# A decoder layer with routed experts on one core: shared experts of three batches moved into the last sorting, first group's tiles and joins moved forward

## The chip, the core and the metric

One core of a Trainium2 chip runs the whole kernel in one launch. The metric is device time in microseconds. The engines are named as the profile names them: PE (TensorE, the matrix engine), DVE (VectorE), ACT (ScalarE), POOL (GpSimd) and SP (SyncE, which here only issues DMAs). Each engine works through its own instructions in order; waits between engines go through semaphores.

## The reference, cut to what matters

Eight batches of 512 tokens with 256 features, float32. Three sublayers, each with a layernorm before it and a residual add behind it:

```python
x = x + attn(layernorm(x))            # one weight vector per head, rolled over the rows, causal
x = x + xattn(layernorm(x), ctx, ctx) # causal softmax attention over a context
x = x + ffn(layernorm(x))

# ffn, on tokens t:
out     = sum over 2 shared experts of (silu(x @ wg_s) * (x @ wu_s)) @ wd_s
probs   = softmax(x @ router_w)                       # 16 routed experts
weights = the two largest of probs, normalized to sum 1
out    += sum over the two chosen experts e of weight_e * (silu(x @ wg_r[e]) * (x @ wu_r[e])) @ wd_r[e]
```

The batches are independent of each other everywhere. The change touches only the order of work in the last sublayer, and some buffers.

## The kernel before, in words

**Batches.** A loop over the eight batches emits, for batch b, the "back" of b (attention's products, projection, second layernorm, scores, softmax, attention, third layernorm, logits, router), interleaved by a list written out by hand (`ORDER`) with the "front" of b + 1 and with what is left of b - 1: its shared experts (steps `h0`, `h1`, `d0`, `d1`, from `steps_shared`), its ranking (`rk`) and its sends (`sd0` to `sd7`). `shared[b]` ends with the residual held in a buffer `x`; for batches of the first group it is also stored to DRAM (`kept`).

**Routing.** The batches form two groups, `GROUPS = ((0, 1, 2, 3, 4), (5, 6, 7))`. For each batch, `ranked` (`rk`) works out on DVE the row that each token takes in its expert's list, and each `send` (L588) is one scatter by POOL of 128 rows to a list in DRAM, `xg`. After the last batch of a group, `tiled` and `tabled` build on DVE and PE the table of tiles of 128 rows: which rows, which expert (`row0`, `far`, `col`). This stretch, from the ranking of the last batch to the first tile loads, is "the sorting".

**Quads.** The routed experts are computed in quads of four tiles, 14 quads for the first group and 10 for the second (`steps_routed`). A quad q is made of: `fetch` (SP loads four tiles, L718), `pick` (ACT copies the gate and up weights of the four tiles' experts, SP and ACT load the down weights `wdn`, L737), `turn` (PE transposes), `hidden` (L772), `down` (L786, then the results `y` times the routing weight on ACT and DVE), and four `put`s (L807), scatters by POOL to `yg` in DRAM. `quads[q]` is a list for a software pipeline: it holds `pick` and `turn` of q + 1, `hidden` of q, `down` of q - 1, `fetch` of q + 3 (q + 4 in the second group), two puts of q - 1 and two of q - 2. So there are two entries more than quads, 16 for the first group.

**Joins.** When all puts of a group are done, `steps_join` makes the output for each batch: `keep` loads the stored residual (`xj`, L842; the first group only), `take` loads the two results of each token (`yj`, L851, two loads of 512 KB), `join` adds both on DVE (L860, two adds over 128 x 1024) and stores to `out` (L861). The buffers of `keep` alternate between two tags with one buffer each (`xn1`, `ctxT`); those of `take` have the tags `qT` and `v2`, two buffers each, so two batches can be in flight.

**Where the quads and joins lie.** `merged` interleaves lists evenly, each step at its share of its list; `idle(n)` puts n empty steps into a list to shift what is behind them. The first group's quads 0 to 11 are merged into the steps of batches 5, 6 and 7 (`lead` is 5): entries 0 to 4, 5 to 8, and 9 to 11. Behind the loop, the sorting of the second group is merged with the remaining entries 12 to 15, the shared experts of batches 6 and 7, and the first six steps of the first group's joins. The rest of those joins is merged with the second group's quads, and the joins of the second group come last. The emitted order is not the final one on each engine: the framework's scheduler orders the instructions anew within the limits of data and buffers, but stays near the emitted order.

Of the kernel before, what the change touches and what calls it, by code (L numbers as in the profile page):

```python
# [25 lines left out]
NSH = 2  # L26

GROUPS = ((0, 1, 2, 3, 4), (5, 6, 7))

XW = D + 2  # L30
FAR = float(1 << 16)
# [41 lines left out]
def decoder_layer(ctx: ExitStack, tc: tile.TileContext, x, ctxT, waT, wvT, woT, bo, wkT, xwv, wqT, wr, wg, wu, wd, out):  # L73
# [634 lines left out]
    def steps_routed(g):  # L708
# [13 lines left out]
        def pick(q):  # L722
            def f():
                wgu = sb.tile([P, QT, 2, KC, MR], F32, tag="wgu", bufs=2, name=f"wgu{g}_{q}")
                es = loaded(G, "act", mybir.EngineType.Activation, G["col"][:, q * QT:(q + 1) * QT], (NE - 1) * MR)
                for i, e in enumerate(es):
                    G["act"] = nc.scalar.copy(wgu[:, i], wgu_r[:, :, :, bass.ds(e, MR)]).ins  # L727

                wdn = sb.tile([P, QT // 2, D], F32, tag="wdn", bufs=3, name=f"wdn{g}_{q}")
                for eng, name, engine, i0, cols in (  # L730
                    (nc.scalar, "act", None, 2, es[2:]),
                    (nc.sync, "sp", mybir.EngineType.SP, 0, G["col"][:, q * QT:q * QT + 2]),
                ):
                    if engine is not None:
                        cols = loaded(G, name, engine, cols, (NE - 1) * MR)
                    for i, e in enumerate(cols):
                        G[name] = eng.dma_start(out=wdn[i * MR:(i + 1) * MR, i0 // 2, :], in_=wdn_d[bass.ds(e, MR), :]).ins  # L737
                G["wgu", q], G["wdn", q] = wgu, wdn
            return f
# [94 lines left out]
    def steps_join(g):  # L834
# [10 lines left out]

        def take(bi):
            def f():
                y = [sb.tile([P, NT, D], F32, tag=tag, name=f"yj{GROUPS[g][bi]}_{tag}") for tag in ("qT", "v2")]
                for r in range(2):
                    rows = r * G["n"] + bi * S  # L850
                    nc.sync.dma_start(out=y[r], in_=G["yg"][rows:rows + S, :].rearrange("(p c) d -> p c d", c=NT))  # L851
                G["yj", bi] = y
            return f
# [30 lines left out]
    def iteration(b):  # L884
# [8 lines left out]
        ends = b == GROUPS[0][-1]  # L893
        order = ORDER.split() + (["rk", *[f"sd{i}" for i in range(8)]] if ends else [])

        late = ("-h0", "-h1", "-d0", "-d1") if b == B - 1 else ()
        return [x[n] for n in order if n in x and n not in late and not (b == GROUPS[1][0] and n[:3] in ("-rk", "-sd"))]

    def flat(x):
        return [f for y in x for f in y]  # L900
# [2 lines left out]
    old = [keeps[0], takes[0]]  # L903
    for i in range(len(keeps)):
        if i + 1 < len(keeps):
            old += [keeps[i + 1], takes[i + 1]]
        old.append(joins[i])
    lead = GROUPS[0][-1] + 1
    for b in range(B):
        if b + 2 < B:  # L910
# [2 lines left out]
        if b == lead:  # L913
            now = merged(now, first[:1] + idle(4) + first[1:-1] + idle(18) + first[-1:] + flat(quads[:5]))
        elif b == lead + 1:
            now = merged(now, flat(quads[5:9]))
        elif b == lead + 2:
            now = merged(now, flat(quads[9:12]))
        for f in now:
            f()  # L920
        if b == 0:
            load_blank()
        if b == 1:
            load_experts()
    last, sh6, sh7 = backs[B - 1], shared[B - 2], shared[B - 1]
    send = [last[f"sd{i}"] for i in range(8)]
    gap = flat(quads[12:])
    sh = [x[n] for x in (sh6, sh7) for n in ("h0", "h1", "d0", "d1")]
    sorting = [last["rk"], *idle(1), *send, first1[0], *idle(0), *first1[1:-1], *idle(2), first1[-1]]
    for f in merged(sorting, gap + sh, [*idle(6), *old[:6]]):  # L930
        f()
    keeps, takes, joins = steps_join(1)
    for f in merged(flat(quads1), old[6:]):
        f()
    for f in [*keeps, *takes, *joins]:
        f()


# [52 lines left out]
```

## Time and profile before

| | |
|---|---|
| three runs | 575.97, 581.40, 585.55 us, median 581.4 |
| the profiled execution | 578.12 us, of which 576.4 us are the span of its instructions |
| PE busy | 508.3 us, 88% of the span |
| DVE busy | 373.1 us, 65% |
| ACT busy | 190.9 us, 33% |
| POOL busy | 229.2 us, 40% |
| DMA | 106.62 MB, on average 185 GB/s |
| mean granted clock of PE | 0.954 of full speed |

The share of busy time is an average over stages with different limits. The stages at issue are the last ones. Times from the span's start: the ranking and sorting of the second group lie between about 449 and 476 us, its quads between 484 and 551 us, its puts between 498 and 558 us, and its joins from 559 us to the end.

A row of a group reads: line, engine, operation, what is written from what, count, then busy time, mean duration in ns of one, and the idle time of the engine just before them with what ended it. A row of a timeline reads: start, duration, engine, line, operation, and in brackets the idle time before it and what ended that. "SPq" and "ACTq" are DMA issues of SP and ACT.

### The profile page before, as it was taken

The page shows a single profiled execution, that of the slowest core. Times are in us where ns is not written, and L with a number is a line of the kernel's source. Part 1 is how long each engine was busy: PE and PEld are TensorE (multiplying, and loading weights), DVE is VectorE, ACT ScalarE, POOL GpSimd, SP SyncE. Part 2 cuts the span into 40 slices and gives each one's busy share as a digit, 9 for nine tenths or more (in the row PEclk, how much of TensorE's full clock was granted, in tenths as well). Part 3 has the DMA queues.
Part 4 walks back from the last instruction along what each step waited for, and adds up shares of the span by engine and source line. Part 5 has one row for each costly group of instructions (what it writes and reads, how often), then busy time and mean ns, then how long its engine had stood idle before and what let it go on. Part 6 is the DMA issues. An engine that isn't in the chain of part 4 may idle for free. (4 is left out here: it accounts for less than half of the span.)

```text
span 576.4 us, 10034 instructions
## 1 busy us (share of the span) xinstructions
PE 508.3 (88%) x3172; PEld 335.4 (58%) x3172; DVE 373.1 (65%) x1290; ACT 190.9 (33%) x483; POOL 229.2 (40%) x257
## 2 busy tenths in 40 slices
PE   7989988999999999999799999999898978977810
PEld 5546626756666665673566757676555645845610
DVE  4358749868769768787577568764865753645325
ACT  2233213332332324231445344443333311635300
POOL 3300504432440540634205363743275671357650
PEclk9999999999999999999799999999999979979855
DMA  8870370851580391294359574496221147788947
GB/s 275 278 300 4 94 281 28 276 211 57 169 325 40 138 340 75 104 314 182 105 158 334 171 236 124 129 327 194 89 103 63 43 155 220 249 252 261 280 129 285
DMA packets 63820, 106.62 MB, mean 185 GB/s; under 512 B 8869, under 2 KB 37551, under 8 KB 63666
## 3 DMA queue, kind: packets, MB, share of 16 engines
q1 hardware_dynamic: 51528, 83.35, 44.1%
q0 software_dynamic: 7680, 16.87, 8.1%
q10 hardware_dynamic: 4560, 5.77, 3.0%
q8 instruction: 25, 0.41, 0.3%
q14 instruction: 27, 0.22, 0.1%
HBM read 81.82 MB, written 33.85 MB: 201 GB/s over the span
## 5 line engine op out<-in xcount | busy, mean ns | idle before, releaser
L807 POOL DMA_INDIRECT yg<-y,to x96 | 96.5, 1006 | 101.2 <-ACT y L797 61.5
L240 POOL TENSOR_TENSOR rs<-ve,power 128x2 f32<-128x2 f32 x48 | 35.3, 743 | 173.7 <-DVE ve L239 173.5
L588 POOL DMA_INDIRECT xg<-row,place x64 | 64.9, 1013 | 24.9 <-issue 16.5
L398 PE MATMUL pc<-T,vh 128*32 128x256 f32 (+1 forms) x512 | 57.8, 490 | 3.7 <-DMA T<-zd 2.3
L772 PE MATMUL pgu<-xsT,wgu 128*64 128x128 f32 x768 | 55.1, 285 | 4.6 <-DVE rh L776 3.2
L772 PEld LDWEIGHTS pgu<-xsT,wgu 128*64 128x64 f32 x768 | 44.2, 141 | 15.8 <-issue 12.7
L450 PE MATMUL psc<-kT,qT 128*128 128x128 f32 (+3 forms) x128 | 40.4, 440 | 0.7 <-DVE kT L261 0.7
L225 DVE BATCH_NORM_STATS2 bn<-x 128x6 f32<-128x256 f32 x96 | 37.6, 413 | 4.2 <-DMA x<-in_x_dram 3.2
L479 PE MATMUL pa<-v,pT 128*128 128x256 f32 x160 | 40.3, 382 | 0.0
L786 PE MATMUL py<-wdn,rh 64*128 64x256 f32 x192 | 35.7, 437 | 5.2 <-DMA wdn<-wdn_d 4.8
L398 PEld LDWEIGHTS pc<-T,vh 128*32 128x32 f32 x512 | 18.5, 109 | 35.1 <-issue 19.7
L631 PE MATMUL pd<-wd_sb,h 128*128 128x256 f32 x128 | 36.1, 412 | 3.2 <-DVE h L619 2.3
L338 PE MATMUL pv<-wv_sb,xr 128*128 128x272 f32 (+1 forms) x128 | 34.1, 413 | 4.0 <-ACT xr L331 4.0
L727 ACT COPY wgu<-wgu_r 128x256 f32 x96 | 32.7, 403 | 11.6 <-DVE col L706 7.6
L479 PEld LDWEIGHTS pa<-v,pT 128*128 128x128 f32 x160 | 29.1, 190 | 10.7 <-issue 4.0
L753 PE MATMUL pxt<-ident,xs 128*128 128x128 f32 x192 | 29.6, 284 | 5.8 <-DMA xs<-xg 3.3
L244 DVE TENSOR_SCALAR xn<-x,mv,rs 128x256 f32<-128x256 f32 x64 | 28.1, 476 | 7.2 <-POOL rs L240 6.4
L799 DVE TENSOR_SCALAR y<-py,w 128x256 f32<-128x256 f32 x48 | 22.3, 478 | 15.6 <-ACT y L797 14.5
L614 PE MATMUL pg<-x2T,wg_sb 128*128 128x512 f32 x64 | 31.6, 598 | 0.0
L338 PEld LDWEIGHTS pv<-wv_sb,xr 128*128 128x128 f32 x128 | 24.7, 199 | 10.5 <-ACT xr L331 6.1
L614 PE MATMUL pu<-x2T,wu_sb 128*128 128x512 f32 x64 | 30.4, 592 | 0.0
L354 PE MATMUL pq<-ctxT,qk_sb 128*128 128x512 f32 x64 | 30.4, 594 | 0.0
(174 smaller groups left out, 911.9 us busy)
## 6 DMA issues: line engine op xcount, KB each, us to landing
T<-zd SPq DMA_DIRECT2D x32, 1024.0 KB
xs<-xg SPq DMA_DIRECT2D x96, 129.0 KB
x<-in_x_dram SPq DMA_DIRECT2D x8, 512.0 KB
ctxT<-in_ctxT_dram SPq DMA_DIRECT2D x8, 512.0 KB
yj_qT<-yg SPq DMA_DIRECT2D x8, 512.0 KB
yj_v<-yg SPq DMA_DIRECT2D x8, 512.0 KB
xg<-blank SPq DMA_DIRECT2D x6, 516.0 KB
wdn<-wdn_d ACTq DMA_DIRECT2D x48, 64.0 KB
```

The costliest lines, as they stand in the source:

```text
L225: nc.vector.bn_stats(stats["bn"][:, c, :], src[:, c, :])
L240: st[b].setdefault(("pow", n), []).append(nc.gpsimd.tensor_tensor(stats["rs"][:, lo:hi], ve[:, lo:hi], power[:, lo:hi], ALU.pow).ins)
L338: nc.tensor.matmul(pv[:, :w], xr[:, k, i, :], wv_sb[:, k, :w], start=(k == 0), stop=(k == KC - 1))
L398: nc.tensor.matmul(s["pc"][o][32 * g:32 * g + 32, 2 * jp * P:], vh[:, jp, h, :], s["T"][h // HPT][:, h % HPT, :S - 2 * jp * P], start=(jp ...
L450: nc.tensor.matmul(pc[:, :w], s["qT"][:, k, i * P:w], s["kT"][:, k, :w], start=(k == 0), stop=(k == KC - 1))
L479: nc.tensor.matmul(pa[:, :D], s["pT", i][:, j * P:(j + 1) * P], s["v2"][:, j, :], start=(j == 0), stop=(j == i))
L588: ins = nc.gpsimd.indirect_dma_start(out=grp[g]["xg"][:, :], out_offset=bass.IndirectOffsetOnAxis(ap=s["place"][:, r, c:c + 1], axis=0), i ...
L614: nc.tensor.matmul(p, w[:, k, mt * P:(mt + 1) * P], s["x2T"][:, k, :], start=(k == 0), stop=(k == KC - 1))
L631: nc.tensor.matmul(pd[:, i, :], s["h", mt][:, c * P:(c + 1) * P], wd_sb[:, mt, :], start=(mt == 0), stop=(mt == NSH - 1))
L772: nc.tensor.matmul(p[o * MR:(o + 1) * MR, n, j, :], wgu[:, i, n, k, :], xT[:, k, i, :], start=(k == 0), stop=(k == KC - 1))
L786: nc.tensor.matmul(py[o][:, j, :], h[o * MR:(o + 1) * MR, j, :], wdn[o * MR:(o + 1) * MR, j, :], start=True, stop=True)
L807: ins = nc.gpsimd.indirect_dma_start(out=G["yg"][:, :], out_offset=bass.IndirectOffsetOnAxis(ap=G["to", q][:, i:i + 1], axis=0), in_=G["y" ...
```

## The change

Five things change in the order and two in the buffers.

1. The shared experts of batch 5 no longer run in the steps of batch 6: with those of batches 6 and 7 they are emitted in the last sorting (`LATE`).
2. Entries 5 to 10 of the first group's quads are merged into batch 6 (before, 5 to 8), entries 11 to 15 into batch 7 (before, 9 to 11). No entry is left for the sorting.
3. All joins of the first group are merged into the sorting; before, six of their steps were, and the rest went with the second group's quads. Within their list, each join has three empty steps ahead of it, and the next take comes behind the join.
4. The second group's quads are emitted alone.
5. The empty steps in the sorting's own list are placed differently.
6. In the second group, the down weights of odd quads take buffers of the tag `h` (three, used by the shared experts until then), those of even quads the tag `wdn` (three) alone.
7. The take of the last batch has its own buffers, of the tags `xn1` and `ctxT`.

```diff
+LATE = (5, 6, 7)
...
-                wdn = sb.tile([P, QT // 2, D], F32, tag="wdn", bufs=3, name=f"wdn{g}_{q}")
+                wdn = sb.tile([P, QT // 2, D], F32, tag="h" if g and q % 2 else "wdn", bufs=3, name=f"wdn{g}_{q}")
...
-                y = [sb.tile([P, NT, D], F32, tag=tag, name=f"yj{GROUPS[g][bi]}_{tag}") for tag in ("qT", "v2")]
+                tags, bufs = (("xn1", "ctxT"), 1) if g and bi == 2 else (("qT", "v2"), 2)
+                y = [sb.tile([P, NT, D], F32, tag=tag, bufs=bufs, name=f"yj{GROUPS[g][bi]}_{tag}") for tag in tags]
...
-        late = ("-h0", "-h1", "-d0", "-d1") if b == B - 1 else ()
+        late = ("-h0", "-h1", "-d0", "-d1") if b - 1 in LATE else ()
...
         if i + 1 < len(keeps):
-            old += [keeps[i + 1], takes[i + 1]]
-        old.append(joins[i])
+            old += [keeps[i + 1]]
+        old += [*idle(3), joins[i]]
+        if i + 1 < len(keeps):
+            old += [takes[i + 1]]
...
         elif b == lead + 1:
-            now = merged(now, flat(quads[5:9]))
+            now = merged(now, flat(quads[5:11]))
         elif b == lead + 2:
-            now = merged(now, flat(quads[9:12]))
+            now = merged(now, flat(quads[11:16]) + idle(0) + old[:0])
...
-    last, sh6, sh7 = backs[B - 1], shared[B - 2], shared[B - 1]
-    send = [last[f"sd{i}"] for i in range(8)]
-    gap = flat(quads[12:])
-    sh = [x[n] for x in (sh6, sh7) for n in ("h0", "h1", "d0", "d1")]
-    sorting = [last["rk"], *idle(1), *send, first1[0], *idle(0), *first1[1:-1], *idle(2), first1[-1]]
-    for f in merged(sorting, gap + sh, [*idle(6), *old[:6]]):
+    last = backs[B - 1]
+    sh = [shared[b][n] for b in LATE for n in ("h0", "h1", "d0", "d1")]
+    sorting = [last["rk"], *[last[f"sd{i}"] for i in range(8)], first1[0], *idle(2), *first1[1:-1], *idle(4), first1[-1]]
+    for f in merged(sorting, flat(quads[16:]) + sh, old[0:]):
+        f()
+    for f in flat(quads1):
         f()
     keeps, takes, joins = steps_join(1)
-    for f in merged(flat(quads1), old[6:]):
-        f()
-    for f in [*keeps, *takes, *joins]:
+    for f in [*takes, *joins]:
         f()
```

`quads[16:]` is empty, as are `old[:0]` and `idle(0)`.

## The prediction

> **What bounds the kernel now.** I read the page's groups first, then the chain that ended last, then GpSimd's (POOL's) timeline and the windows of the last 140 us. TensorE is busy 508.3 of 576.4 us; of its 68 us of idle time some 29 lie behind its last matmul and some 20 between 440 and 540. So the end is a string of handovers, and its longest stretch is a queue of scatters on POOL.
>
> ```profile
> L807 POOL DMA_INDIRECT yg<-y,to x96 | 96.5, 1006 | 101.2 <-ACT y L797 61.5
> L588 POOL DMA_INDIRECT xg<-row,place x64 | 64.9, 1013 | 24.9 <-issue 16.5
> ```
>
> Each put (`yg<-y,to`) and send (`xg<-row,place`) holds POOL for 1.01 us. The timeline of POOL gives the pace and the fixed points:
>
> ```profile
> 419.06 0.72 POOL L240 TENSOR_TENSOR rs<-ve,power 128x2 f32<-128x2 f32 x1 [1.09 <-DVE ve L239]
> ...
> 436.02 0.74 POOL L240 TENSOR_TENSOR rs<-ve,power 128x2 f32<-128x2 f32 x1
> ...
> 444.56 0.75 POOL L240 TENSOR_TENSOR rs<-ve,power 128x2 f32<-128x2 f32 x1
> ...
> 463.00 0.96 POOL L588 DMA_INDIRECT xg<-row,place  x1 [0.31 <-DVE begin L668]
> ...
> 498.32 0.97 POOL L807 DMA_INDIRECT yg<-y,to  x1 [20.04 <-ACT y L797]
> 499.60 0.97 POOL L807 DMA_INDIRECT yg<-y,to  x1 [0.30 <-issue]
> ```
>
> Start to start is 1.28 us. 419.06 is batch 7's second layernorm, 436.02 and 444.56 are the two halves of its third; the row at 436.02 has no idle time before it: a put had just ended, so POOL itself was the limit. Batch 7's sends start at 463.00 and the second group's puts at 498.32. The last of its 40 puts starts at 556.88: 58.6 us where 39 steps of 1.28 make 49.9. **8.7 us are gaps**, and the chain names what they wait for (start, us, what):
>
> ```profile
> 500.66 8.26 DMA xs<-xg
> ...
> 528.29 5.06 DMA wdn<-wdn_d
> ...
> 556.88 2.05 DMA yg<-y,to
> 558.94 0.34 SPq L851
> ```
>
> Loads that elsewhere take 2.7 us take 8.26 and 5.06 here, and the windows (us, busy times, PEclk, DMA share, GB/s) say why:
>
> ```profile
> 444.00:452.00 8.00, 6.02 (x43) 3.49 (x45) 3.49 (x11) 2.26 (x7) 4.54 (x6) 1.00 0.16 59
> ...
> 504.00:508.00 4.00, 0.88 (x8) 0.43 (x6) 3.13 (x5) 2.29 (x7) 3.08 (x4) 1.00 0.95 310
> ...
> 528.00:532.00 4.00, 1.67 (x26) 1.22 (x22) 2.86 (x4) 1.71 (x5) 3.39 (x3) 1.00 1.00 367
> ```
>
> The DMA engines are full while the second group runs, because the first group's joins share them, and nearly idle at 444 to 452, just ahead of the sorting.
>
> **Batches 6 and 7.** Batch 5's shared experts leave batch 6's steps: by the groups at L614 and L631, (31.6 + 30.4 + 36.1) / 8 = 12.3 us of TensorE. Two more quads come in: (55.1 + 29.6 + 35.7) / 24 = 5.0 us each. TensorE was full there, so batch 7's second layernorm moves by 10.0 - 12.3, and as VectorE limits part of it I take **-2 us**. In batch 7's steps five entries replace three, but they hold three `hidden` as before, one `down` more and one `turn` less: nothing on TensorE. On POOL it differs. In the compiled order the sends of batch 6 and eight puts (quads 11, 12) now stand between the second layernorm and the first half of the third, where eight sends and four puts stood. Four more at 1.28 us are 5.1 us, and there is no idle time to take them. The second half comes behind quad 13's four puts: 4 x 1.28 + 0.7 + 0.6 + the normalizing's 1 is about 7.5 us, less than the 8.5 before. Sum: the router of batch 7 (first VectorE operation at 449.60) starts 5.1 - 1.0 - 2 = **2 us later**, at 451.7. Ends: -2 if VectorE hides the puts, +5 if quad 13's results come late.
>
> **The sorting.** What is queued now:
> - SP. The first load of a second-group tile stood behind two join loads; now it stands behind 17 DMAs of the joins (ten `yj`, three `xj`, four stores), each waiting in order. At about 0.5 us an issue they cost 8.5 us of a queue that was idle. Their data take longer. The first take waits for quad 13's last put, at 436.0 - 2 + 5.1 + 2.3 + 3 x 1.28 = 445.3, plus 2.1 us (before: put 461.72, load 463.83): issue at 447.4. Then the chain store 0, `xj` 2, store 1, `xj` 3, store 2, `xj` 4 is serial, since `xj` 2 reuses the buffer that store 0 empties.
> - VectorE. Its compiled order puts joins 0 and 1 around the router's first operations, join 2 inside the ranks, join 3 in the tile table and join 4 ahead of `far` and `col`. A join is two adds of 1.22 us, so a join that waits for its load holds the router. Before, one half join stood in the tile table only.
>
> What does a 512 KB transfer take? The rows: 3.5 us for `yj` at the tail (558.94 to the add at 562.40), 4.1 us beside the sends, 5.3 us for a store under load, 8.26 us for a load in full traffic. The Trainium skill, "DMA: Bandwidth & Descriptors", section "Anatomy of one DMA — SWDGE (gpsimd) path", has 2.0 us plus bytes / 436 GB/s for a transfer issued by GpSimd, an estimate of 3.2 us here[...]. By the rule, join 2's data come at 447.4 + 3.2 + 2.4 (join 0) + 3.2 (store 0) + 3.2 (`xj` 2) = 459.4; by the rows, with 3.5 for loads and 5.3 for the store, at 462.1. VectorE reaches join 2 near 463. By both it isn't late, but by the rows 1 us is left, not 4, and I take the rows.
> Joins 0 and 1 land at 451 to 455: VectorE waits for them and adds 4.9 us, of which I count **3 us** behind 451.7 (the router's gaps take the rest). Join 2's 2.4 us come whole. The `h` and residual operations that now stand between the ranks' steps replace quads' operations, about even. Places, 460.6 before, come at 460.6 + 2 + 3 + 2.4 = 468. There is one gain: before, ready places waited until 463.0 because POOL was still at puts; now no puts are left. So the sends start at 468.2, **5.2 us later**. They take 11.5 us and land 2.4 us later, at 482; joins 3 and 4 end by then (out to 478), and SP is free at about 472.
> TensorE has the three shared experts (37 us by the rows above) for this time, where it had two and some quads; its end isn't what is late.
>
> **The second group.** The four tile loads land 5.2 us later (last one near 494.5, not 489.3). `down` of quad 0 stands behind `turn` of quad 3 on TensorE, so it moves from 495.8 to 497, and the first put from 498.3 to **499.5**. From there POOL has 39 steps of 1.28 us, 49.9 us, against 5.0 us of TensorE and 5.1 of POOL per quad, so the puts set the pace. The joins' traffic (four batches of 2 MB) is gone; 3 MB of tiles, 2.5 MB of weights and 3 MB of results stay, half of what the engines carried. Six weight buffers in place of three let loads start a quad earlier; I cost this with the gaps: 1.6 of the 8.7 us stay. Ends: 0, or all 8.7 if the tiles' own buffers cause them. Last put: 499.5 + 49.9 + 1.6 = 551.0, before 556.9: **-5.9 us**.
>
> **The end.** From 557.85 it is 18.5 us. The third take was issued at 563.65 and 565.01, behind its buffers, and its last add began at 570.94. With buffers of its own it is issued by 561.5, but 3 MB at the 293 GB/s of this stretch need over 10 us: **-1.4 us**. Ends: 0 and -3.
>
> Sum: 576.4 - 5.9 - 1.4 = 569.1 us of span. The profiled run took 578.12, 1.7 over its span: 570.8. The median shown, 581.4, is 1.0057 of that run: **574.0**, 1.3% below. Runs lie between 576 and 585.6, so 2% is about what a measurement of this kernel can tell from no change.
>
> **Rivals.**
> - *The sorting costs nothing* (0.34). POOL's backlog is hidden and the joins' data come ahead of VectorE. For it: DMA is at a share of 0.16 there. Against: 436.02 has no slack. TensorE then decides: from 447.6 three shared experts, four `turn` and two `hidden`, some 45 us, then `y`: first put at 495, last with no gaps at 544.9, end 18.1 later, span 563: **567.9**.
> - *Slower: SP and VectorE in lockstep* (0.14). If each transfer takes the 8.26 us of the loaded row, join 2's data come at 447.4 + 8.3 + 2.4 + 8.3 + 8.3 = 475; joined at 477.5, places 479, sends out at 490.5, landed 493, tiles at 506, first put 508.5, last 560, span 578: **583**; over 593 if sends and tile loads, in the same traffic, take three times as long too. It decides from a first put later than 506.8 (498.3 + 7.1 of gaps + 1.4 at the end). For it: 8.5 MB of joins in the sorting at 290 GB/s are 30 us.
> - *The gaps stay* (0.12): the second group's loads wait for tile buffers, not for traffic. Span 576.4 + 1.2 - 1.4 = 576.2: **581**. For it: TensorE ran three quads ahead by 504. Against: 367 GB/s at 528.
> - The forecast has 0.40, by itself 570 to 578.
>
> A clock loss lies beside all of these: after TensorE's idle 466.2 to 469.6 the granted clock was 0.50 until 475, some 3 us lost. A wait of VectorE on a join that starves TensorE would bring it again; TensorE's slack in the sorting covers one.
>
> Range: 565 to 585 takes in all four. Faster by over 2% (under 569.8) is most of the first rival and an edge of the forecast: 0.35. Slower by over 2% (over 593) is the lockstep with slow sends and tile loads, most of its 0.14: 0.11. The rest is 0.54.
>
> **What would show it.** Right: the third layernorm's first half some 3 us later, sends at 466 to 470, DMA share above 0.7 between 448 and 475 and below 0.6 after 500, puts at a steady 1.28 us, three takes in a row. Wrong: VectorE waiting over 5 us for a `yj` or `xj`, SP reaching the second group's tiles after the sends landed, or puts with gaps though DMA is free.

## The result, and the profile after

The changed kernel takes 576.58 us, the kernel before 583.11 us (medians of 20 runs each): a ratio of 0.993, with an interval from 0.990 to 0.996. (Ratios compare the means of each kernel's faster runs, those within 1.5% of its fastest, here 13 of the 20 before and all 20 after; the medians of all runs would give 0.989.) In a second comparison, on a chip of the same pace, it was 0.989 (0.984 to 0.993). The forecast was 0.987. The sign was right, and the size came to half of it in the first comparison.

The profiled execution has a span of 574.8 us; before it was 576.4. That of the changed kernel is at its median (576.5 us), that of before is one of its faster ones (578.1 us, where the median is 583.1). So the places below differ by less than the times do, and where a typical execution of the kernel before spends the other 5 us, no profile shows.

The places at which the forecast can be checked (us from the span's start; the last column is a second profile of the changed kernel, d_after, from the second comparison):

| | before | forecast | after | after, d_after |
|---|---|---|---|---|
| batch 7, second layernorm, first half | 419.1 | 417 | 423.5 | 422.8 |
| batch 7, third layernorm, first half | 436.0 | 439.1 | 445.5 | 444.8 |
| batch 7, third layernorm, second half | 444.6 | 446.7 | 452.8 | 452.2 |
| router of batch 7, first VectorE operation | 449.6 | 451.7 | 458.6 | 457.9 |
| first send of batch 7 | 463.0 | 468.2 | 474.2 | 473.9 |
| first put of the second group | 498.3 | 499.5 | 503.3 | 503.1 |
| from first to last put of it | 58.6 | 51.5 | 52.0 | 51.9 |
| from the last put's start to the end | 19.5 | 18.1 | 19.5 | 18.1 |

First the page's groups of the changed kernel (line, engine, operation; busy time and mean ns of one; idle time before it and what ended that), then POOL's timeline:

```profile
L809 POOL DMA_INDIRECT yg<-y,to x96 | 94.8, 987 | 80.6 <-ACT y L799 40.2
L590 POOL DMA_INDIRECT xg<-row,place x64 | 63.5, 992 | 44.0 <-DVE whole L663 26.4
```

```profile
423.50 0.72 POOL L242 TENSOR_TENSOR rs<-ve,power 128x2 f32<-128x2 f32 x1 [1.44 <-DVE ve L241]
...
445.49 0.75 POOL L242 TENSOR_TENSOR rs<-ve,power 128x2 f32<-128x2 f32 x1
...
452.78 0.74 POOL L242 TENSOR_TENSOR rs<-ve,power 128x2 f32<-128x2 f32 x1
...
474.23 1.06 POOL L590 DMA_INDIRECT xg<-row,place  x1 [19.26 <-DVE whole L663]
...
503.32 1.00 POOL L809 DMA_INDIRECT yg<-y,to  x1 [18.75 <-ACT y L799]
504.62 0.99 POOL L809 DMA_INDIRECT yg<-y,to  x1 [0.30 <-DVE y L801]
```

A put or send costs POOL as much as before. The puts' idle time before them fell by 20 us, from 101.2 to 80.6, and the sends' rose by 19 us: POOL now stands still for 19.26 us ahead of the first send, since it has no puts left and the places come late. The windows (us, busy times, PEclk, DMA share, GB/s) at the places shown of before:

```profile
444.00:452.00 8.00, 5.83 (x23) 3.58 (x23) 4.17 (x12) 1.78 (x4) 5.76 (x8) 0.79 0.02 1
504.00:508.00 4.00, 3.59 (x40) 2.32 (x36) 1.86 (x5) 2.44 (x7) 3.09 (x4) 1.00 0.74 225
528.00:532.00 4.00, 3.59 (x32) 2.14 (x31) 1.96 (x6) 2.45 (x7) 2.85 (x3) 1.00 0.83 255
```

The DMA engines are less full while the second group runs (0.74 and 0.83, where 0.95 and 1.00 stood), and TensorE is busy there for 3.59 of 4 us, where it was for 0.88 and 1.67. The chain's end:

```profile
555.31 2.06 DMA yg<-y,to
...
559.69 9.54 DMA yj_ctxT<-yg
...
569.33 1.22 DVE x L863
```

The last batch's take is issued at 559.69, where before it was issued by 565.01. But its data now take 9.54 us, where 5.83 us were enough, so the last add starts only 1.6 us earlier than before, as much as the last put does.

So the second group's stretch is 6.6 us shorter, as forecast, and it starts 5.0 us later, where 1.2 us were forecast. **What has to be explained lies ahead of the router**: the second layernorm of batch 7 is 4.4 us late, and it should have been 2 us early. Behind it the forecast's own steps hold to 2.2 us each.

Two theories. **Q**: in batches 6 and 7 the puts fill POOL's queue, the 0.74-us power operation of a layernorm waits behind them, and TensorE idles for it. **W**: the work moved into these batches is more than what was moved out of them. Two more theories are about what follows: that the joins hold the router, and that the joins' place or the buffers make the gaps between the puts.

### The profile page after: what moved, and what is told of

Same layout as the page of the kernel before. It is cut to its first block, busy times and chain, and to the rows that moved or that the text cites. A ratio compares the mean times of both kernels' runs of the same rounds, so it can differ in the third digit from the quotient of the medians.

```text
span 574.8 us, 10013 instructions
## 1 busy us (share of the span) xinstructions
PE 509.4 (89%) x3172; PEld 332.8 (58%) x3172; DVE 372.6 (65%) x1290; ACT 190.9 (33%) x483; POOL 226.1 (39%) x257
## 5 line engine op out<-in xcount | busy, mean ns | idle before, releaser
L809 POOL DMA_INDIRECT yg<-y,to x96 | 94.8, 987 | 80.6 <-ACT y L799 40.2
L590 POOL DMA_INDIRECT xg<-row,place x64 | 63.5, 992 | 44.0 <-DVE whole L663 26.4
L774 PE MATMUL pgu<-xsT,wgu 128*64 128x128 f32 x768 | 60.0, 285 | 3.4 <-DVE rh L778 3.0
L774 PEld LDWEIGHTS pgu<-xsT,wgu 128*64 128x64 f32 x768 | 45.0, 140 | 17.4 <-issue 12.3
L481 PE MATMUL pa<-v,pT 128*128 128x256 f32 x160 | 42.8, 401 | 2.2 <-DVE pT L472 2.2
L481 PEld LDWEIGHTS pa<-v,pT 128*128 128x128 f32 x160 | 30.5, 199 | 13.1 <-issue 3.8
L400 PEld LDWEIGHTS pc<-T,vh 128*32 128x32 f32 x512 | 18.7, 109 | 33.5 <-issue 17.7
L633 PE MATMUL pd<-wd_sb,h 128*128 128x256 f32 x128 | 34.4, 400 | 3.2 <-DVE h L621 2.0
L755 PE MATMUL pxt<-ident,xs 128*128 128x128 f32 x192 | 31.3, 285 | 2.9 <-DMA xs<-xg 2.1
L258 PE MATMUL pt<-ident,xn 128*128 128x128 f32 x128 | 23.7, 289 | 7.1 <-DVE xn L246 4.1
L788 PE MATMUL py<-wdn,rh 64*128 64x256 f32 x192 | 29.6, 404 | 0.4 <-PE py L788 0.4
```

What stands on the lines that cost most here:

```text
L400: nc.tensor.matmul(s["pc"][o][32 * g:32 * g + 32, 2 * jp * P:], vh[:, jp, h, :], s["T"][h // HPT][:, h % HPT, :S - 2 * jp * P], start=(jp ...
L481: nc.tensor.matmul(pa[:, :D], s["pT", i][:, j * P:(j + 1) * P], s["v2"][:, j, :], start=(j == 0), stop=(j == i))
L590: ins = nc.gpsimd.indirect_dma_start(out=grp[g]["xg"][:, :], out_offset=bass.IndirectOffsetOnAxis(ap=s["place"][:, r, c:c + 1], axis=0), i ...
L633: nc.tensor.matmul(pd[:, i, :], s["h", mt][:, c * P:(c + 1) * P], wd_sb[:, mt, :], start=(mt == 0), stop=(mt == NSH - 1))
L755: nc.tensor.transpose(pt[:, i * P:(i + 1) * P], xs[:, i, 2 + k * P:2 + (k + 1) * P], ident)
L774: nc.tensor.matmul(p[o * MR:(o + 1) * MR, n, j, :], wgu[:, i, n, k, :], xT[:, k, i, :], start=(k == 0), stop=(k == KC - 1))
```

## The experiments

The runs fell on chips of two kinds. On one kind the kernel before takes 582 to 583 us; both profiles of the table are from there, and so are d_after, e8, e9 and e10. On the other kind it takes 627 to 634 us; there all other runs were made. Ratios are always to the kernel before on the same chip, and places are compared within one kind.

**Controls.** The kernels themselves, unchanged.

> The changed kernel itself, as a control: the four runs before this were on a chip on which the kernel before takes 631 us, not 583. If the change is worth on this chip what it was worth in the first comparison, the ratio to the kernel before is 0.990 to 0.996 again. If the second group's loads, whose issues on SP with an address from a register run slower here (some 7 us per quad where it was 5), set the pace of the second group in place of the puts, then the 7 us that the puts' stretch had gained are not to be had: ratio 0.996 to 1.006, first to last put longer than 58 us.

> The kernel before itself, for its trace on this chip. Expected if SP's issues with addresses from registers make the difference between the chips: the same places as in the first trace up to 257 us (the second batches have none of these), then 7 us later by the first group's sorting at 294, 20 to 25 us later by batch 7's second layernorm, and 25 to 30 us more behind it.

> The changed kernel once more, beside the next three on one chip, because the chips differ by 1% and the changed kernel was measured on another chip than the kernels with the joins back. If the joins in the sorting cost some 1.3% on these chips: ratio to the kernel before 0.993 to 0.999 here, and at least 0.008 above the kernels with the joins back. If the chips made that difference: 0.980 to 0.988.

On a chip of the second kind the changed kernel comes to 0.996 (0.994 to 0.999), on one of the first to 0.989 (0.984 to 0.993). The kernel before loses its time there where the first group's sorting and its quads run: batch 5's second layernorm is 8 us late (295.2 for 287.5), batch 7's 23 us, and the second group's puts take 70.0 us from first to last. They take 70.2 us with the change, with idle time between the puts of 20 us both times, at a DMA share of 0.25 to 0.7 until 588. So on this kind the change's main gain is not to be had. SP's issues are not the cause, which I had expected: four tile loads take it 1.9 us on both kinds. Engines stand idle with nothing in the trace to end it. The same instruction in the two profiles of the kernel before (first kind, then second):

```profile
273.85 0.58 ACT L413 ACTIVATE late<-pc,half 128x384 f32<-128x384 f32 x1 [2.80 <-PE pc L398]
```

```profile
281.66 0.58 ACT L413 ACTIVATE late<-pc,half 128x384 f32<-128x384 f32 x1 [4.38 <-remote]
```

Its only wait is for TensorE, whose matmuls for it are recorded as done at 276.3. What it waited for after that stays open, and so does the difference of the chips.

**One part of the change at a time.** The shared experts of batch 5 alone (f1), the quads alone (f2), the buffers alone (e8), each on the kernel before:

```diff
 f1
-        late = ("-h0", "-h1", "-d0", "-d1") if b == B - 1 else ()
+        late = ("-h0", "-h1", "-d0", "-d1") if b - 1 in (5, 6, 7) else ()
-    sh = [x[n] for x in (sh6, sh7) for n in ("h0", "h1", "d0", "d1")]
+    sh = [x[n] for x in (shared[5], sh6, sh7) for n in ("h0", "h1", "d0", "d1")]
 f2
-            now = merged(now, flat(quads[5:9]))
+            now = merged(now, flat(quads[5:11]))
-            now = merged(now, flat(quads[9:12]))
+            now = merged(now, flat(quads[11:16]))
-    gap = flat(quads[12:])
+    gap = []
 e8
-                wdn = sb.tile([P, QT // 2, D], F32, tag="wdn", bufs=3, name=f"wdn{g}_{q}")
+                wdn = sb.tile([P, QT // 2, D], F32, tag="h" if g and q % 2 else "wdn", bufs=3, name=f"wdn{g}_{q}")
+                tags, bufs = (("xn1", "ctxT"), 1) if g and bi == 2 else (("qT", "v2"), 2)
```

> The kernel before with one part of the change alone: the shared experts of batch 5 run in the last sorting. It takes 12.3 us of TensorE out of batch 6 and adds nothing there. The prediction counted them in full, so batch 7's second layernorm 12 us earlier (407 on a chip of the first kind, where before has 419); on a chip of the second kind a kernel with the buffers as well had it 7 us earlier. The 12.3 us come back in the sorting, where TensorE then has 16 puts' worth of quads and three shared experts: first put of the second group no earlier, ratio 0.990 to 1.000. If TensorE were free enough in batch 6 for the rest to be hidden: layernorm 5 us earlier or less.

> The kernel before with another part alone: six quad entries in batch 6, five in batch 7, none in the sorting; shared experts, buffers and the joins' entries as before. If each quad costs its 5.0 us of TensorE: batch 7's second layernorm 10 us later than before (429). If the puts on POOL and the half clock behind them add to it: 12 to 16 us later, and the shared experts' move can't give that back. The joins can begin when the last put is out, so takes from 458 to 465 and no gaps in the second group's puts even so: first to last put 50 to 53 us. Ratio 0.985 to 0.995.

> The kernel before with the change's buffers alone (down weights of odd quads of the second group in the tag h, own buffers for the last take); no step is moved. With the joins back, both the quads' move and the shared experts' move could be undone in turn and 1.2 to 1.6% stayed. If the buffers carry that: ratio 0.982 to 0.990, the second group's puts with gaps 2 to 5 us smaller and the end 1 to 1.5 us shorter. If the moves carry it, each for the other: 0.994 to 1.001.

And with one part undone in the changed kernel: batch 5's shared experts (e4: `LATE = (6, 7)`), the joins' place (e3 and e5), that and the quads' place (e6), the joins' place and batch 5's shared experts (e7), the joins' place and the buffers (e10):

```diff
 e3, e5 (also in e6, e7, e10)
-    for f in merged(sorting, flat(quads[16:]) + sh, old[0:]):
+    for f in merged(sorting, flat(quads[16:]) + sh, [*idle(6), *old[:6]]):
...
-    for f in flat(quads1):
+    for f in merged(flat(quads1), old[6:]):
 e6: flat(quads[5:9]), flat(quads[9:12]) and, in the sorting, flat(quads[12:]) + sh
 e7: LATE = (6, 7)
 e10: tag="wdn"; tags, bufs = ("qT", "v2"), 2
```

> The changed kernel, but the shared experts of batch 5 run in batch 6's steps again (12.3 us of TensorE). Theory Q (POOL's queue is the limit in batches 6 and 7, and TensorE idles behind it): a part of the 12.3 us fills TensorE's idle time, layernorms of batch 7 later by 4 to 8 us and POOL's backlog shorter: no wait of VectorE for POOL above 2 us in batch 6; sends at 478 to 482. Rival W (TensorE's work is the limit): all of batch 7 later by 11 to 12.3 us, sends at 485. In the sorting TensorE then has 12.3 us less; as its end isn't what is late there, nothing comes back. Ratio to the kernel before 1.000 to 1.007 under Q, 1.010 to 1.016 under W.

> The changed kernel, but the first group's joins lie where they did before the change: the first six entries of their list at the end of the sorting, the rest merged with the second group's quads. If the joins' traffic makes the gaps between the second group's puts: first to last put takes 57 to 60 us again instead of 52.0, router to places 11 us instead of 15.2, sends start near 470, first put 499 to 501, last put near 558, ratio to the kernel before 0.995 to 1.003. If the gaps had gone through the shared experts' move or the weights' six buffers instead: first to last put stays 51 to 54 us, and with the sends 4 us earlier the ratio is 0.984 to 0.989.

> The changed kernel with the first group's joins where they were before the change, a second time, so that the next two stand beside it on one chip. On the chips of the last runs this was 0.981 of the kernel before where the changed kernel was 0.996. If the joins in the sorting are what eats the gain on every chip, the ratio is 0.977 to 0.987 again; if the first result came from that chip alone, 0.990 to 1.000.

> As e5, and in addition the first group's quads lie as before the change (entries 5 to 8 in batch 6, 9 to 11 in batch 7, 12 to 15 in the sorting): what is left of the change is the shared experts of batch 5 in the sorting and the buffers. Theory Q (the quads' puts on POOL delay batches 6 and 7): second layernorm of batch 7 no later than before, its second half with less than 1.5 us between its variance on VectorE and the power on POOL (2.6 with the change), layernorms 4 to 9 us earlier than in e5; but POOL has 16 puts left in the sorting, so sends 2 to 4 us behind the places. Ratio 0.975 to 0.985. Rival W (TensorE's whole work up to the sorting decides): 12.3 us less in batch 6, all of it seen at batch 7's second layernorm; then 16 puts and five quads' worth of work in the sorting: ratio 0.985 to 0.998.

> As e5, and in addition the shared experts of batch 5 run in batch 6 again: what is left of the change is six quad entries in batch 6 and five in batch 7, and the buffers. If the shared experts' place does not matter because TensorE idles in batch 6 (e4 showed the third layernorm of batch 6 no later with 12.3 us more of TensorE): within 0.4% of e5. If TensorE decides: 0.010 to 0.020 above e5.

> As e5 (joins back), but without the change's buffers: what is left is the quads' and the shared experts' move. If the buffers carry the gain: 0.994 to 1.001; if the moves do: 0.981 to 0.988.

The stretch that the failed step is about, from batch 6's second layernorm to batch 7's (first halves, us):

| second kind of chip | quads | shared experts | stretch | ratio to before |
|---|---|---|---|---|
| c_before | as before | as before | 71.3 | 1 |
| f1 | as before | moved | 65.9 | 0.995 (0.991 to 0.998) |
| e6 | as before | moved | 64.9 | 0.984 (0.979 to 0.989) |
| f2 | moved | as before | 76.4 | 0.987 (0.983 to 0.991) |
| e7 | moved | as before | 76.4 | 0.988 (0.984 to 0.993) |
| e4 | moved | as before | 76.2 | 0.991 (0.989 to 0.994) |
| c_after | moved | moved | 74.7 | 0.996 (0.994 to 0.999) |
| e3, e5 | moved | moved | 75.6, 77.8 | 0.981 (0.976 to 0.986), 0.984 (0.980 to 0.988) |

Two of the ends that the table starts from, in POOL's timelines of f1 and of f2:

```profile
435.24 0.72 POOL L240 TENSOR_TENSOR rs<-ve,power 128x2 f32<-128x2 f32 x1 [2.23 <-DVE ve L239]
```

```profile
448.83 0.72 POOL L240 TENSOR_TENSOR rs<-ve,power 128x2 f32<-128x2 f32 x1 [0.64 <-issue]
```

Moved alone, the shared experts shorten the stretch by some 6 us; moved alone, the quads lengthen it by 5. (f1 and f2 ran on another chip than c_before, and e3 and e5, the same kernel on two chips, differ by 2.2 us.) With the quads in place, moving the shared experts too gives 74.7 to 77.8, where 76.2 to 76.4 stand without it: nothing that can be told from the spread. **The two terms do not add.** My sum had them as 12.3 and 10.0 us of one full engine. On this kind TensorE isn't full there: in c_after it stands idle for 3.3 us up to 388 and for 3.5 us up to 392. On the first kind, where it is nearly full, neither move was run alone; there the stretch takes 59.6 and 58.8 us with the steps unmoved (before, e8), and 63.1, 61.8, 63.1 and 61.5 us with both moved (the changed kernel, d_after, e9, e10).

The ratios of f1, f2, e5, e6 and e10 came as one of the theories had them; e3 and e4 came out better than any had, and e7 and d_after lie between their two. Several ratios on the second kind are better than that of the whole change. They come from four chips, so whether the joins' place costs something there (0.996 against 0.981 and 0.984) is not settled: no run of the changed kernel shares a chip with e3 or e5. On one chip of the first kind there is no such difference: e10 has 0.986 (0.981 to 0.991), d_after 0.989 (0.984 to 0.993), with intervals that overlap. And e8, the buffers alone, has 1.001 (0.998 to 1.005), with 60.5 us from first to last put: **the buffers close no gap**. 

e10 shows what does. It emits the joins as late as before and has the old buffers, and yet its puts have no gap at all (first and last of the second group, POOL's timeline; then windows as above):

```profile
502.49 1.00 POOL L809 DMA_INDIRECT yg<-y,to  x1 [18.97 <-ACT y L799]
...
552.80 0.98 POOL L809 DMA_INDIRECT yg<-y,to  x1 [0.30 <-issue]
```

```profile
452.00:460.00 8.00, 7.96 (x34) 3.46 (x32) 5.93 (x12) 1.98 (x5) 1.30 (x2) 1.00 0.69 262
...
468.00:476.00 8.00, 7.22 (x24) 4.06 (x23) 7.70 (x24) 0.60 (x1) 2.16 (x2) 1.00 1.03 345
...
508.00:516.00 8.00, 6.78 (x64) 5.19 (x61) 2.74 (x7) 3.24 (x9) 6.17 (x7) 0.81 0.77 230
```

50.3 us for 39 steps is 1.29 us each. The DMA engines are full from 468 as in the changed kernel, since the five takes are issued between 453.0 and 472.5 here, and between 453.3 and 473.0 in d_after: the framework's scheduler brings the takes forward to the same place, wherever they were emitted. In the kernel before the takes are issued at 463.8, 486.0, 499.0, 524.0 and 540.7. Three puts of the first group stand behind batch 7's sends until 477.3, and from the second take on they stand in SP's order behind the first sixteen tile loads, which SP issues until 485.9. In e10 the last of these puts is at 450.9, and that is the quads' move. The other kind says which of the two moves it is: in f2, with the quads' move alone and the joins' list of before, the last put of the first group is at 480.1 and all five takes go out from 482.2 to 503.3, ahead of the second group's loads; in f1, with the shared experts' move alone, they go out from 493.9 to 581.3, as spread out as before. First and last take in SP's queue, in e10, f2 and f1:

```profile
453.00 0.34 SPq L854 DMA_DIRECT2D yj_qT<-yg  x1
...
472.49 0.88 SPq L854 DMA_DIRECT2D yj_v<-yg  x1
```

```profile
482.25 0.34 SPq L851 DMA_DIRECT2D yj_qT<-yg  x1
...
503.30 0.61 SPq L851 DMA_DIRECT2D yj_v<-yg  x1
```

```profile
493.94 0.34 SPq L851 DMA_DIRECT2D yj_qT<-yg  x1
...
581.31 0.45 SPq L851 DMA_DIRECT2D yj_v<-yg  x1
```

**Half of the joins** in the sorting (e9: `old[:16]` there, `old[16:]` with the second group's quads).

> The changed kernel, but only the first 16 of the 30 entries of the joins' list (two joins and three takes) lie in the sorting, the rest with the second group's quads. If each join in the sorting costs its share (traffic beside the sends and tile loads): halfway between all and none of them moved, 0.986 to 0.992. If only the joins that end beside the sends and the tile loads cost (2, 3 and 4): as good as none moved, 0.979 to 0.986.

0.986 (0.981 to 0.991), no gaps, takes at 454.2 to 474.9. That lies on the border of both expectations, and both had lost their ground: the scheduler puts the joins where they were with the whole list.

**POOL's queue.** e1 holds eight puts back behind the power operation in each of the two batches, f3 only those that stood right ahead of it:

```diff
+    def behind(now, b, half, qs):
+        puts = [grp[0]["put", q, n] for q in qs for n in range(4)]
+        now = [f for f in now if f not in puts]
+        i = now.index(backs[b][("at1", "at3")[half]]) + 1
+        def held(f):
+            def g():
+                with tc.issue_after(st[b]["pow", 3][half]):
+                    f()
+            return g
+        return now[:i] + [held(f) for f in puts] + now[i:]
 e1: behind(now, b, 0, (6, 7)) in batch 6; behind(now, b, 1, (12, 13)) in batch 7
 f3: behind(now, b, 0, (7,)) in batch 6; behind(now, b, 0, (12,)), behind(now, b, 1, (13,)) in batch 7
```

> The changed kernel, but in batch 6 the eight puts of quads 6 and 7 may be issued only behind the first half of the third layernorm's power operation on POOL, and in batch 7 those of quads 12 and 13 only behind the second half. The same work, another order on POOL. Theory Q (the puts queued ahead of the 0.74-us power operation on POOL hold the layernorms, TensorE then waits and comes back at half clock): the first half of batch 6's third layernorm goes from 387.6 back to 385 or earlier, batch 7's second from 423.5 to 416-419, its third from 445.5/452.8 to 434-438/440-444, the waits of VectorE of 3 to 4 us for POOL are gone, sends start at 466-470 instead of 474.2; the puts come later, so the first joins' take moves to 455 or so; the time falls by 4 to 8 us against the changed kernel (ratio to the kernel before 0.980 to 0.987). Rival W (it is the work itself of TensorE and VectorE that was moved into batches 6 and 7): layernorms within 1.5 us of the changed kernel's, ratio 0.991 to 0.996. Rival D (the joins' data and the joins on VectorE hold the sorting whatever comes ahead): layernorms earlier as under Q, but sends at 473 to 475 and ratio 0.990 to 0.996.

> The changed kernel, with only those puts held back that stood right ahead of the third layernorm on POOL: quad 7's four behind the first half in batch 6, quad 12's behind the first half and quad 13's behind the second in batch 7. Theory Q, on a chip of the first kind: the 3.3 us between variance and power in batch 6 and the 2.5 to 3.9 in batch 7 go to under 0.6; no idle TensorE and no half clock at 390; second half of batch 6's third layernorm at 393 to 396 instead of 400 to 401, batch 7's second layernorm at 418 to 420 instead of 423, third at 436 to 440; the last put 2 to 5 us later than it would be, still ahead of the router; sends at 466 to 470 instead of 474; time 4 to 7 us less than the changed kernel: ratio 0.977 to 0.984. Rival W: layernorms within 1.5 us of the changed kernel's, ratio 0.986 to 0.994. Rival Y (held puts keep the results' buffers, and quads wait for those): second half of batch 6's third layernorm later than 400, ratio above 0.995.

Both are slower: 1.010 (1.007 to 1.013) and 1.005 (1.003 to 1.008). POOL's timeline of e1, batch 6's third layernorm, and two of its waits between 405 and 432, then c_after's wait for the second of these two (who waited for whom: us in total, times, longest; "remote" is a wait that nothing in the trace ends):

```profile
407.75 0.72 POOL L242 TENSOR_TENSOR rs<-ve,power 128x2 f32<-128x2 f32 x1 [18.97 <-DVE ve L241]
429.12 0.72 POOL L242 TENSOR_TENSOR rs<-ve,power 128x2 f32<-128x2 f32 x1 [4.71 <-DVE ve L241]
```

```profile
ACT y L799 <- DMA yg<-y,to: 3.9, 2, 3.5
ACT xsT L758 <- remote: 9.9, 1, 9.9
```

```profile
ACT xsT L758 <- PE pxt L755: 3.8, 1, 3.8
```

POOL is idle for 18.97 us and the first half is not earlier (407.28 in c_after), because on this kind of chip no queue stood there: in c_after POOL itself waits 1.75 us for the variance. And the second half comes 8.5 us later than in c_after (420.62). Some 3.5 us of this are a wait for `y`, the results' buffers, which come free only when a put has landed: that is rival Y of f3, but seen in e1. Most of the rest is a wait of ScalarE and VectorE that nothing in the trace ends (9.9 us, where c_after waits 3.8 us for TensorE). f3 has no wait for `y` there, only one of the second sort (6.8 us), and its second half comes 3.7 us later than in c_after. So why both are slower is shown in part only, and these two runs say nothing on what the queue costs on a chip of the first kind; no run of them fell there.

e7b measures the price of a hold itself, in the kernel before:

```diff
+        if n == 3 and b in (6, 7) and lo == 0:
+            held = sb.tile([P, P], F32, tag="held", bufs=1, name=f"held{b}")
+            for i in range(12):
+                hold = nc.gpsimd.tensor_copy(held, ve[:, lo:lo + 1].to_broadcast([P, P])).ins
+            late = tc.issue_after(hold)
```

> The kernel before, with twelve small copies (some 0.3 us each, an estimate from 0.61 us for a copy of four times as many elements) on POOL between the variance and the power operation of the first half of the third layernorm in batches 6 and 7: about 3.5 us of POOL each time, which is what the queue of puts cost in the changed kernel (3.3 and 2.5 us). Nothing else is changed. Theory Q: each hold delays what follows by its length and more, since TensorE idles and then runs at half clock: the second half of batch 6's third layernorm 4 to 6 us later, sends 7 to 11 us later, time 1.009 to 1.017 of the kernel before. Rival W (TensorE has other work and the hold is hidden): sends less than 3 us later, ratio 0.997 to 1.004.

POOL's timeline of e7b, batch 6, and of c_before at the same place:

```profile
403.01 4.26 POOL L244 COPY held<-ve 128x128 f32<-128x128 f32 x12
407.23 0.72 POOL L247 TENSOR_TENSOR rs<-ve,power 128x2 f32<-128x2 f32 x1
...
413.03 0.69 POOL L247 TENSOR_TENSOR rs<-ve,power 128x2 f32<-128x2 f32 x1 [3.63 <-DVE ve L239]
```

```profile
404.14 0.74 POOL L240 TENSOR_TENSOR rs<-ve,power 128x2 f32<-128x2 f32 x1
411.56 0.69 POOL L240 TENSOR_TENSOR rs<-ve,power 128x2 f32<-128x2 f32 x1 [5.23 <-DVE ve L239]
```

Counted from the first half's turn on POOL (403.01, where the hold begins; 404.14 in c_before), the second half comes after 10.0 us, where c_before has 7.4: of a hold of 4.26 us, 2.6 us arrive. In batch 7 it is 10.9 us for 10.0. The time is 1.003 (1.001 to 1.006) of before: two holds, 8.5 us together, cost 2.1 us (0.4 to 3.7 by the interval). That is W's range, though not nothing: **a hold on POOL costs about a quarter of its length here, and at most some 45%**, not its length and more, as Q had it.

**The joins on VectorE.** e2 lets the joins' adds begin only behind batch 7's ranking; f4 is f3 with that.

```diff
-                        nc.vector.tensor_tensor(x, x, y[r], ALU.add)
+                    with tc.issue_after(st[B - 1]["ranked"]) if g == 0 else nullcontext():
+                        nc.vector.tensor_tensor(x, x, y[r], ALU.add)
```

> The changed kernel, but the adds of the first group's joins may be issued on VectorE only behind the ranking of batch 7, so router and ranks are free of them. From the router's first VectorE operation to the places was 11.0 us before the change and is 15.15 with it. If the joins inside the router and the ranks cost those 4.1 us: places and first send 4 us earlier (470 instead of 474.2), but joins end later and their buffers too, so the takes and stores of batches 2 to 4 fall beside the second group's loads; the first put then 2 to 4 us earlier or, if that traffic is worth more, no earlier, and gaps of 1 to 5 us come back between the puts: ratio to the kernel before 0.985 to 0.995. If the joins' adds only fill gaps of VectorE there (rival): sends within 1 us of 474.2, ratio 0.993 to 1.000.

> As f3, and in addition the adds of the first group's joins only behind batch 7's ranking, as in e2. Up to the router as f3. From the router's first VectorE operation to the first send 9 to 11 us instead of 16; the joins end later, their loads and stores fall beside the second group's first tile loads. If nothing is given back: 3 to 4 us less than f3. If it is given back, as e2 on a chip of the second kind showed (sends 7 us nearer to the router, then 3.6 us more from first to last put): as f3 or slower.

In e2 the first send comes 9.0 us behind the router's first VectorE operation, as the first of its two expectations had it, but the ratio is the rival's, 0.998 (0.995 to 1.000). f4 has 1.005 (1.002 to 1.007) beside f3's 1.005, "as f3 or slower". In f4 the router's first VectorE operation is at 490.19, and POOL's timeline goes on:

```profile
499.16 1.82 POOL L591 DMA_INDIRECT xg<-row,place  x1 [7.97 <-DVE row L581]
501.29 1.44 POOL L591 DMA_INDIRECT xg<-row,place  x1 [0.30 <-issue]
503.03 1.52 POOL L591 DMA_INDIRECT xg<-row,place  x1 [0.30 <-DVE whole L664]
```

9.0 us from router to first send, where c_after has 15.9 and f3 18.5. So what the adds cost in the sorting is as much as it seemed. But nothing of it reaches the end: the first put comes 0.5 us earlier than in f3 (541.2 for 541.7), and first to last put takes 74.3 us for 72.2. While the adds go on beside them, the first sends take 1.4 to 1.8 us instead of 1.0; whether the adds are what slows them was not isolated.

## Why the prediction was right or wrong, point by point

- **"Batches 6 and 7", the term of -2 us: wrong, and this is the step that failed.** In the two profiles of the table the second layernorm of batch 7 came 4.4 and 3.7 us late. I added up TensorE's records of d_after and of the kernel before, overlaps counted once, from the same step of batch 5 (330.0 before, 330.6 in d_after) to that layernorm. The windows, before and d_after:

```profile
330.00:419.06 89.06, 87.42 (x685) 59.69 (x685) 62.27 (x223) 37.12 (x93) 42.73 (x46) 1.00 0.57 183
```

```profile
330.60:422.82 92.22, 88.94 (x761) 62.17 (x759) 62.74 (x230) 42.50 (x108) 50.81 (x54) 1.00 0.60 190
```

  Quads: some 11.3 us more (forecast 10.0 for two of them; a third `turn` lies in this stretch too). Shared experts: 10.9 less (forecast 12.3, from means over all batches in which overlapping records count twice). The steps that were not moved: some 1.1 more. (How overlaps are shared out decides this split, not the sum.) All together TensorE is busy for 88.9 us instead of 87.4, 1.5 more, where I had 2.3 less; that is W's side. It stands idle for 3.3 us instead of 1.6. So this stretch, which the forecast has 2 us shorter, is 3.2 us longer: of these 5.2 us some 3.5 are TensorE's sum and 1.7 are waits. (It begins 0.6 us late.) The size of each part is read from this pair of profiles; no run on this kind of chip takes one part alone away.
- **The wait that I had not looked for in batch 6.** I counted POOL's queue in batch 7 only. Batch 6 got eight more puts too. The timeline of the changed kernel, first kind of chip:

```profile
384.08 0.17 DVE L241 TENSOR_SCALAR ve<-mv 128x2 f32<-128x2 f32 x1
...
386.58 0.98 POOL L809 DMA_INDIRECT yg<-y,to  x1 [0.30 <-issue]
387.56 0.74 POOL L242 TENSOR_TENSOR rs<-ve,power 128x2 f32<-128x2 f32 x1
388.34 0.74 DVE L246 TENSOR_SCALAR row<-x,mv,rs 128x256 f32<-128x256 f32 x2 [4.09 <-POOL rs L242]
...
390.02 2.47 PE L481 MATMUL pa<-v,pT 128*128 128x256 f32 x5 [2.25 <-DVE pT L472]
```

  The variance is there at 384.25, the power operation starts 3.3 us later behind three puts, VectorE waits for it 4.09 us with the copy `pT` behind it in its order, and TensorE stands still for 2.25 us. The trace shows this chain; that it is worth about 2 us at the end of the stretch is argued from TensorE's idle time, and so Q is not ruled out as this part of the delay. e7b measures less for such a hold on the other kind of chip, and no run takes it away on this one.
- **POOL's count in batch 7, +4.1 us to the router: right.** From second layernorm to router it took 30.5 us before, 35.1 with the change, 35.1 in d_after: 4.6 more. The steps between, 22.1 and 7.5 us, came out as 22.0 and 7.3.
- **The sorting, 16.5 us from router to first send: right** (15.6 and 16.0). VectorE never waited over 0.7 us for a join's data, so the rival of a lockstep fell; SP was free when the sends had landed. That the joins cause the delay is shown by f4. For join 2's data the Trainium skill, "DMA: Bandwidth & Descriptors", section "Anatomy of one DMA — SWDGE (gpsimd) path", gave 459.4 and the rows 462.1, from a first take at 447.4. With the take at 453.3 (d_after), 5.9 us later, that is 465.3 and 468.0. Join 2 began at 468.9, after a wait of 0.64 us for `xj`: the rows were right to 0.9 us, the rule 3.6 us short, and the 1 us of slack was used up. (The rule is for transfers that GpSimd issues; these are SP's.) The last take's 9.54 us, with six such loads in flight, is three times the 3.2 us of the rule. Two signs that I had named did not come: the DMA share is 0.02 until the first take at 453.9, which had to wait for the late puts, and after 500 it is 0.74 and 0.83, not below 0.6. I had half of the traffic gone; 225 and 255 GB/s of 310 and 367 are left, some 70%.
- **The second group, gaps from 8.7 to 1.6 us: right in size and in mechanism** (52.0 and 51.9 us; the traffic is gone from there), **wrong in which part does it.** Neither the joins' emitted place nor the six weight buffers, but the quads' move, which lets the joins run before the second group's loads (e10 and e8 here; f2 and f1 on the other kind). The quads' move alone was not run on this kind.
- **The end, -1.4 us: right, though the profile of the first comparison doesn't show it.** From the last put's start to the end, twelve of the fourteen profiles with own buffers for the last take have 18.0 to 18.7 us, the six without 19.4 to 20.1. That first profile, with 19.5, is one of the two exceptions.
- **From span to time: luck.** The last factor of the forecast, 1.0057 from the profiled execution to the median, did not hold for the changed kernel, whose profiled execution took its median. The forecast span was 5.7 us too short (569.1 for 574.8), the forecast time only 2.6 us (574.0 for 576.6): the factor hid some 3 us of the error.
- **The rival "the sorting costs nothing" fell** with the first send at 474.2; "the gaps stay" fell on this kind of chip, and is what happens on the other.

No version tried is clearly better than the changed kernel on one chip. e10, which has only the quads' and the shared experts' move, is as good, with fewer edits.

## What to carry to other kernels

Two moves whose effects lie in one stretch are not a sum of busy times: measure each alone and both, as f1, f2 and the changed kernel do here (-6, +5, and together +3). When steps are moved, count every queue of every batch they pass, POOL's short operations behind long scatters too, and weigh a wait by what else its engines have to do. And where a scheduler reorders, ask which dependence lets a step start, not where it is emitted.

## What the runs showed of the hardware that was not expected

Equal idle time of TensorE did not cost the same clock. After the same 2.25 us of idle time at 390, the clock was granted at half for 3.4 us in the first profile of the changed kernel and not at all in the second (windows of the first, then of d_after; the third figure from the end is the granted clock):

```profile
388.00:400.00 12.00, 9.98 (x62) 8.28 (x64) 5.87 (x17) 2.35 (x6) 4.90 (x6) 0.86 0.77 249
```

```profile
388.00:400.00 12.00, 9.75 (x76) 7.89 (x75) 4.82 (x15) 3.32 (x7) 5.57 (x7) 1.00 0.80 261
```

e9's clock was halved there too, e10's was not, and from batch 6's second layernorm to batch 7's the two with the half clock took 63.1 us, the two without 61.8 and 61.5. More weight has that two kinds of chips run the same program 8% apart, alike to 2 us up to 252 us, and that an edit's worth differs between them.
